# A state-space scan rewritten: scanning h + x·B, diagonals of B on VectorE, convolution taps on VectorE

## The chip, the core and the metric

The kernel runs on one core of a Trainium2 chip as a single launch. The metric is the device time of that launch in microseconds (us). The core's engines run side by side, each with its own queue in a fixed order: TensorE (PE; PEld is its weight load), VectorE (DVE), ScalarE (ACT), GpSimd (POOL), and SyncE (SP), which only issues DMA here. An engine that reaches an instruction whose input is not ready stands still, and so does everything behind it in its queue.

## What is computed

Two layers, each with a sequence mixer and a feed-forward part, over 8 sequences of 256 tokens with 128 features. Only the first mixer changes. It is a selective state-space block (D = 256 channels, N = 16 states per channel, K = 4 taps):

```python
Xn = layernorm(X)
X_main = Xn @ W_up1.T                                  # (b, l, 256)
X_main = silu(causal_depthwise_conv(X_main, conv_w, K=4) + conv_b)
pp = X_main @ W_ll.T + b_ll
delta = softplus(pp[..., :D]); Bm = pp[..., D:D+N]; Cm = pp[..., D+N:]
A = -exp(A_log)                                        # (D, N)
A_bar = exp(delta * A)
U = X_main * (A_bar - 1) / (delta * A) * delta * Bm    # = X_main * Bm * (A_bar - 1) / A
H[t] = A_bar[t] * H[t-1] + U[t]                        # for each of D x N states
Y[t] = sum over n of Cm[t, n] * H[t, :, n]
out = X + (Y * silu(Xn @ W_up2.T)) @ W_down.T + b_down
```

After it come an expert-choice feed-forward part (8 experts, 512 tokens each), a retention layer with 8 heads, and a top-2 feed-forward part over 16 weight banks.

## The kernel before, in words

**Setup.** x is loaded and normalized and turned into `XnT` (features on the partitions, tokens along the free axis, three zero columns ahead of each sequence). The convolution is folded into the up projection: GpSimd multiplies W_up1 by each tap into `wcv` (line 242), and the four products are added up by TensorE. `eye` is the 64-column identity in both halves of the partitions; `dg` holds diagonals of 1/A.

**front(q), lines 303 to 410,** prepares a block of two sequences (512 tokens), in pieces that `yield`. First the convolution: for each of two channel chunks `dc` and each sequence `h`, four matmuls into `pu` (L314), which ScalarE moves to `xm` (L318). Then the gate (L327), the projections for delta (L353, `pd`) and for B and C (L364, `pbc`), softplus through Exp and Ln, the transposed B (`pbt` L383 to `BT` L388) and the transposed x (`pxT` L393 to `xT` L401, and with its halves swapped by DMA, `xS`). Delta is put together by a subtraction on GpSimd (L406) and an addition on VectorE (L408), both with two operands in SBUF. C goes to DRAM and comes back broadcast over all partitions as `Cb` (L644).

**The loop over 64 units** (line 787 on) walks b (8 sequences), g (4 groups of 4 states) and dc (2 channel chunks). Each unit k is a tile of 128 channels x 4 states x 256 tokens, and passes through:

- `spread_b` (L657, GpSimd, one (b, g) ahead by four units): `Bd` = `eye` times B, two instructions for each (b, g), so that a matmul of x with it spreads x·B over the tokens
- `x_times_b` (L673, TensorE): 8 matmuls, x·B into PSUM as `u`
- `decays` (L684, ScalarE): `ab` = exp(delta·A), four instructions
- `steps` (VectorE): L692 makes `u` <- (ab - 1)·u, L694 writes zero into the first decay of each state, and L696 is one scan over all 4 x 256 elements, h <- ab·h + u
- `times_c` (L700, GpSimd): h <- h·C
- `sums` (L709, TensorE): 16 matmuls with `dg` add up the states over n, times 1/A, into `py`
- after 8 units: `gated` (L718, VectorE) and `down` (L726, L733, TensorE), to `ypr`

The order on PE, DVE, ACT and POOL is the order of the program, written out by hand. In iteration k: VectorE gets `steps(k)`; TensorE gets a part of the expert work, `x_times_b(k + 1)`, `sums(k - 2)`; GpSimd gets `times_c(k - 1)` and `spread_b` for unit k + 4 (if dc is 0); ScalarE gets `decays(k + 2)`. Then every generator in `running` gives one piece: `front(1)` to `front(3)` (started at units 0, 16 and 32 by `START`), the threshold search for the experts (`find`: L431 to L453 on VectorE and L444 on TensorE, ten rounds), the residual base (L772, L774 on GpSimd) and the selection of each expert's tokens (`select`: L522 to L531 on VectorE, L535 and L557 on TensorE, indirect gathers L548 on GpSimd). The expert work itself (L606, L624 on TensorE, L611, L629 on ScalarE, indirect scatters L572 on GpSimd) is cut into five parts an expert. `front(0)` runs entirely ahead of the loop, with five rounds of `find` between its pieces. `u` has 2 buffers in PSUM, `ab` 3, `h` 4, and all other matmul results share 2 banks (`bank`).

After the loop comes the second layer (lines 866 on), which the change does not touch.

Of the kernel before, what the change touches and what calls it, by code (L numbers as in the profile page):

```python
# [8 lines left out]
F32 = mybir.dt.float32  # L9
# [3 lines left out]
ALU = mybir.AluOpType  # L13
# [4 lines left out]
NB = 8  # L18
# [28 lines left out]
WB = DI + NH * DM + NH  # L47


@with_exitstack  # L50
def block_kernel(ctx: ExitStack, tc: tile.TileContext, a: dict, out: bass.AP):
# [33 lines left out]
    )  # L85
    ones_b = const.tile([P, P], BF16, name="ones_b")
# [63 lines left out]
    with ExitStack() as l0:  # L150
# [25 lines left out]
        wcv = main.tile([P, K, D], F32, name="wcv")  # L176
# [9 lines left out]
        for q in range(4):  # L186
# [3 lines left out]
        conv_w = main.tile([P, K, D], F32, name="conv_w", tag="Cb", bufs=3)  # L190
        nc.sync.dma_start(
            conv_w.rearrange("p k d -> p (k d)"),
            a["conv_w"].rearrange("k d -> (k d)").partition_broadcast(P),
        )
# [11 lines left out]
        wll = load0("wll", [P, ND, D + 2 * N], a["wll"].rearrange("(c p) e -> p c e", p=P))  # L206
        bll_d = load0("bll_d", [P, ND])
        bll_bc = load0("bll_bc", [2 * N, 1])
# [33 lines left out]
        nc.gpsimd.tensor_tensor(wcv, bc(wup1, 1, K), conv_w, ALU.mult)  # L242
# [58 lines left out]
        gate, delta, xT, BT = {}, {}, {}, {}  # L301

        def front(q):
            cols = slice(q * BLK, (q + 1) * BLK)
            win = slice(2 * q, 2 * q + 2)
            xq = main.tile([P, ND, BLK], F32, name=f"xm{q}", tag="xm")
# [3 lines left out]
            for dc in range(ND):  # L310
                for h in range(2):
                    pu = bank(f"pu{dc}_{h}_{q}", [P, L])
                    for k in range(K):
                        nc.tensor.matmul(  # L314
                            pu, wcv[:, k, dc * P : (dc + 1) * P], XnT[:, 2 * q + h, k : k + L],
                            start=(k == 0), stop=(k == K - 1),
                        )
                    nc.scalar.activation(  # L318
                        xq[:, dc, h * L : (h + 1) * L], pu, AF.Silu if q == 0 else AF.Identity,
                        bias=conv_b[:, dc : dc + 1],  # L320
                    )
                    yield
# [39 lines left out]
            pb = bank(f"pbc{q}", [2 * N, BLK])  # L362
            for kc in range(ND):
# [3 lines left out]
            BC = main.tile([2 * N, BLK], F32, name=f"BC{q}", tag="BC")  # L367
            nc.scalar.activation(BC, pb, AF.Identity, bias=bll_bc)
            nc.sync.dma_start(
                C_d[2 * q : 2 * q + 2].rearrange("b (n l) -> n b l", l=L),  # L370
                BC[N:, :].rearrange("n (b l) -> n b l", l=L),
            )
            yield
            nc.vector.scalar_tensor_tensor(z, w, -1.0, z, ALU.add, ALU.subtract)
# [12 lines left out]
            for rows, at in own:  # L387
                nc.scalar.copy(BTq[rows, :, at], pbt[rows, :, at])  # L388
            for i in range(2):
# [21 lines left out]


# [3 lines left out]
        ready, complete = set(), set()  # L416
# [12 lines left out]
        def search():  # L429
# [66 lines left out]
            G = main.tile([P, 2, NB, E0], F32, name="G")  # L496
# [153 lines left out]
        def spread_b(b, g):  # L650


            t = main.tile([P, 4, 2, BK], F32, name=f"Bd{b}_{g}", tag="Bd", bufs=3)
            j = 4 * (b % 2)
            for i in range(2):
                w = slice(2 * i, 2 * i + 2)
                nc.gpsimd.tensor_tensor(  # L657
                    t[:, w], eye.unsqueeze(1).unsqueeze(1).to_broadcast([P, 2, 2, BK]),
                    bc(BT[b // 2][:, j + 2 * i : j + 2 * i + 2, NG * g + 2 : NG * g + 4], 3, BK),
                    ALU.mult,  # L660
                )
            Bd[b, g] = t

        def x_times_b(k):

            b, g, dc = units[k]
            U[k] = ps_u.tile([P, NG, L], F32, name=f"u{k}", tag="u")
            for c in range(2):
                for half in range(2):
                    for r in range(2):  # L670
# [5 lines left out]
                            Bd[b, g][rows, 2 * c + half], start=True, stop=True,  # L676
                        )

# [10 lines left out]
        def steps(k):  # L689

            hh[k] = main.tile([P, NG, L], F32, name=f"h{k}", tag="h", bufs=4)
            nc.vector.scalar_tensor_tensor(U[k], ab[k], -1.0, U[k], ALU.add, ALU.mult)  # L692

            nc.vector.memset(ab[k][:, :, 0:1], 0.0)  # L694
# [757 lines left out]
```

## Time and profile before

| | |
|---|---|
| median of 3 runs | 685.59 us (685.58 to 686.54) |
| the profiled execution's own time | 684.96 us |
| its span in the trace | 683.1 us |
| PE busy | 544.8 us (80%), mean granted clock 0.873 |
| DVE busy | 432.2 us (63%) |
| POOL busy | 383.8 us (56%) |
| ACT busy | 332.3 us (49%) |
| first and last scan of the loop start at | 67.0 and 418.2 us |

The profile comes from one execution. A group of instructions shows how often it ran, its busy time, the mean of one in ns, and after the second bar how long its engine stood idle ahead of it and whom it waited for. A window row gives, for a stretch of the span, the busy time of each engine with the number of instructions, then the granted TensorE clock, the DMA share and GB/s. An fp32 matmul leaves two records, so L673 shows 1024 for 512 matmuls. Records of one engine can overlap: an instruction that is issued while its predecessor still runs begins, in the record, before it can work.

### The profile page before, as it was taken

Reading aid. Unit: us, or ns where it says so; the run is one execution under the profiler, and the core shown is the slowest. Engines: PE = TensorE matmul, PEld = TensorE weight load, DVE = VectorE, ACT = ScalarE, POOL = GpSimd, SP = SyncE. Lnnn points to the kernel's source line nnn. Section 1 sums busy time; section 2 is a strip of 40 time slices with the busy share of each in tenths; the row PEclk is TensorE's granted clock in tenths of the full one; section 3 lists DMA queues with packets and bytes.
Section 4 is the critical chain, followed back from the end, with each engine's and each line's share of the span. In section 5 each row is a group of like instructions: output and inputs, shape, how many; then the busy total and the mean of one; then the engine's idle time right before and its main releaser. Section 6 shows DMA issues by size and latency. Waiting matters only on the chain.

```text
span 683.1 us, 14527 instructions
## 1 busy us (share of the span) xinstructions
PE 544.8 (80%) x5721; PEld 415.7 (61%) x5721; DVE 432.2 (63%) x669; ACT 332.3 (49%) x763; POOL 383.8 (56%) x320
## 2 busy tenths in 40 slices
PE   0897768779989889979887975496449989999980
PEld 0665645667755668755766764354125589999870
DVE  7377898997955767856868696664027543544423
ACT  2646346447487756587764741362003244555430
POOL 5004565686988789987899896107730023344240
PEclk9996798889999899999999998577558899999995
DMA  7914101232396243332332220124224247889206
GB/s 203 117 25 124 33 32 40 104 95 82 73 204 138 74 115 73 95 93 66 95 91 55 71 71 6 62 93 139 110 81 148 84 151 252 264 292 312 88 30 186
DMA packets 59859, 76.27 MB, mean 112 GB/s; under 512 B 14992, under 2 KB 43808, under 8 KB 59536
## 3 DMA queue, kind: packets, MB, share of 16 engines
q1 hardware_dynamic: 51632, 65.81, 33.6%
q0 software_dynamic: 8160, 9.54, 6.6%
q8 instruction: 45, 0.74, 0.4%
q14 instruction: 22, 0.18, 0.1%
HBM read 59.46 MB, written 13.78 MB: 107 GB/s over the span
## 4 chain that ended last, share of the span: by engine, by line
PE 50%; DVE 20%; issue 9%; ACT 8%; POOL 4%; another core or an unknown queue 4%; DMA 3%; SPq 1%; POOLq 0%; DVEq 0%; ACTq 0%
PE ph L1201 5%; PE py L709 5%; PE py L1215 5%; PE u L673 5%; PE ph L606 4%; DVE h L696 4%; DVE u L692 4%; PE pu L314 4%; PE po L624 2%; PE ps L1034 2%; ACT ab L684 2%; PE pd L353 2%; POOL h L700 2%; DVE st L1041 1%
## 5 line engine op out<-in xcount | busy, mean ns | idle before, releaser
L700 POOL TENSOR_TENSOR h<-h,Cb 128x1024 f32<-128x1024 f32 x64 | 169.5, 2744 | 35.4 <-DVE h L696 20.1
L696 DVE TENSOR_TENSOR_SCAN h<-ab,u 128x1024 f32<-128x1024 f32 x64 | 146.3, 2287 | 5.9
L684 ACT ACTIVATE ab<-delta,An 128x256 f32<-128x256 f32 x256 | 108.5, 497 | 19.4 <-DVE h L696 17.5
L1221 POOL DMA_INDIRECT y_d<-yo,xt x47 | 45.5, 968 | 115.9 <-DVE yo L1220 103.8
L692 DVE SCALAR_TENSOR_TENSOR u<-ab,u 128x1024 f32<-128x1024 f32 x64 | 77.8, 1216 | 37.7 <-PE u L673 18.8
L709 PE MATMUL py<-h,dg 64*64 64x128 f32 x2048 | 79.0, 296 | 18.3 <-POOL h L700 11.3
L673 PE MATMUL u<-Bd,xT 64*128 64x128 f32 x512 | 81.1, 304 | 14.4 <-DVE h L696 12.7
L673 PEld LDWEIGHTS u<-Bd,xT 64*128 64x128 f32 x512 | 68.6, 206 | 25.2 <-issue 9.9
L709 PEld LDWEIGHTS py<-h,dg 64*64 64x64 f32 x2048 | 62.5, 145 | 33.0 <-POOL h L700 17.0
L673 PE MATMUL u<-Bd,xS 64*128 64x128 f32 x512 | 79.4, 305 | 1.7 <-DMA xS<-xT 1.7
L1206 ACT ACTIVATE hid<-ph,wb 128x128 f32<-128x128 f32 x188 | 53.3, 370 | 49.2 <-issue 24.0
L673 PEld LDWEIGHTS u<-Bd,xS 64*128 64x128 f32 x512 | 66.7, 206 | 2.0 <-DMA xS<-xT 2.0
L1041 DVE TENSOR_TENSOR st<-ps,decay_sb 128x384 f32<-128x384 f32 x64 | 31.2, 547 | 53.8 <-remote 27.7
L572 POOL DMA_INDIRECT acc_d<-oc,idx x32 | 51.5, 1609 | 17.0 <-ACT oc L629 8.8
L1150 POOL DMA_INDIRECT xs_d<-xk,pos x32 | 32.1, 1002 | 41.4 <-DVE hit L1132 31.9
L1201 PE MATMUL ph<-xT,wb 128*128 128x128 f32 x376 | 51.5, 281 | 3.3 <-DVE xT L1195 2.7
L657 POOL TENSOR_TENSOR Bd<-eye,BT 128x256 f32<-128x256 f32 x64 | 52.3, 1050 | 0.0
L1215 PE MATMUL py<-wb,hid 128*128 128x128 f32 x376 | 50.2, 278 | 0.0
L1201 PEld LDWEIGHTS ph<-xT,wb 128*128 128x128 f32 x376 | 46.6, 195 | 5.7 <-DVE xT L1195 3.1
L624 PE MATMUL po<-w,ht 128*128 128x128 f32 x256 | 39.5, 296 | 10.8 <-ACT BT L388 2.6
L624 PEld LDWEIGHTS po<-w,ht 128*128 128x128 f32 x256 | 33.7, 199 | 22.1 <-ACT ht L611 8.0
L1215 PEld LDWEIGHTS py<-wb,hid 128*128 128x128 f32 x376 | 46.4, 194 | 0.1
(257 smaller groups left out, 896.6 us busy)
## 6 DMA issues: line engine op xcount, KB each, us to landing
wb<-in_bank_dram SPq DMA_DIRECT2D x47, 514.0 KB
Cb<-C_d SPq DMA_DIRECT2D x32, 512.0 KB
w<-in_w_dram SPq DMA_DIRECT2D x16, 256.0 KB
xs_d<-zrow SPq DMA_DIRECT2D x1, 3031.5 KB
xt<-xs_d SPq DMA_DIRECT2D x11, 260.0 KB
xS<-xT SPq DMA_DIRECT2D x16, 128.0 KB
y<-y_d SPq DMA_DIRECT2D x8, 256.0 KB
decay_sb<-in_decay_dram SPq DMA_DIRECT2D x1, 1536.0 KB
```

Of the source, the lines that this page charges most:

```text
L572: i = nc.gpsimd.indirect_dma_start(out=acc_d, out_offset=bass.IndirectOffsetOnAxis(ap=idx[:, e, s : s + 1], axis=0), in_=oc, in_offset=Non ...
L624: nc.tensor.matmul(po, ht[:, hc, s * P : (s + 1) * P], w2[:, hc, :], start=(hc == 0), stop=(hc == NH - 1),)
L657: nc.gpsimd.tensor_tensor(t[:, w], eye.unsqueeze(1).unsqueeze(1).to_broadcast([P, 2, 2, BK]), bc(BT[b // 2][:, j + 2 * i : j + 2 * i + 2, ...
L673: nc.tensor.matmul(U[k][:, 2 * r : 2 * r + 2, t0 : t0 + BK], xT[b][r ^ half][rows, c, dc * P : (dc + 1) * P], Bd[b, g][rows, 2 * c + half] ...
L684: nc.scalar.activation(ab[k][:, n, :], delta[b // 2][:, dc, (b % 2) * L : (b % 2 + 1) * L], AF.Exp, scale=An[:, dc, g * NG + n : g * NG + ...
L692: nc.vector.scalar_tensor_tensor(U[k], ab[k], -1.0, U[k], ALU.add, ALU.mult)
L696: return nc.vector.tensor_tensor_scan(hf, af, uf, 0.0, ALU.mult, ALU.add)
L700: nc.gpsimd.tensor_mul(hh[k][:, w], hh[k][:, w], Cb[b, g][:, w])
L709: nc.tensor.matmul(pyv[cols, i, dc, :], dg[rows, dc, g * NG + n, :], hh[k][rows, n, j * P : (j + 1) * P], start=(g == 0 and dc == 0 and n ...
L1201: nc.tensor.matmul(ph[:, hc, :], w[:, hc * P : (hc + 1) * P], xTs[t], start=True, stop=True)
L1206: nc.scalar.activation(hids[t][:, hc, :], ph[:, hc, :], AF.Relu, bias=w[:, DI + NH * DM + hc : DI + NH * DM + hc + 1],)
L1215: nc.tensor.matmul(py, hids[t][:, hc, :], w[:, DI + hc * DM : DI + (hc + 1) * DM], start=(hc == 0), stop=(hc == NH - 1),)
```

## The change

It does three things, and moves some pieces to fit them.

1. **Scan.** With G = H + x·B the recurrence becomes G[t] = (G[t-1] + x[t]B[t] - x[t-1]B[t-1])·A_bar[t]. TensorE delivers the step differences directly: `Bd` is now made from `step` (the identity minus the identity shifted by one column), and two small extra matmuls for each unit (8 rows, 2x3 columns) subtract the step across the 64-token edges. `xE` holds what these need: 12 records of matmuls, two ScalarE copies and two small GpSimd products for each block. `steps` is now four scans of 256, add then multiply, with no L692 and no L694. What was added to H is taken out of Y once for each block: sum over n of C·B/A, times x, made by a VectorE product `CB`, a matmul `pq` and a VectorE product for each dc; four more matmuls of `sums` in each unit with g = 0 add it into `py`.
2. **Diagonals of B.** `spread_b` stays on GpSimd for the first 6 (b, g), and goes to VectorE for the other 26.
3. **Convolution.** One up projection (`wup1`, 512 columns) for each dc, and the four taps as four VectorE instructions that read `pu` from PSUM; the first has the bias. `wcv`, its GpSimd product and the broadcast load of the taps are gone.

The last piece of `front` (the `pq` piece) of block 0 runs in the loop; `front(1)` to `front(3)` start two units later; `pbc` has 48 rows rather than 32, so that C begins at row 32.

```diff
+    step = const.tile([P, BK], F32, name="step")
+    nc.vector.tensor_copy(step, eye)
+    nc.vector.tensor_sub(step[:, 1:], step[:, 1:], eye[:, 0 : BK - 1])
+    less = const.tile([P, BLK // BK], F32, name="less")
+    nc.vector.tensor_scalar(less, eye[:, 0 : BLK // BK], -1.0, None, ALU.mult)
...
-        nc.gpsimd.tensor_tensor(wcv, bc(wup1, 1, K), conv_w, ALU.mult)
...
             for dc in range(ND):
-                for h in range(2):
-                    pu = bank(f"pu{dc}_{h}_{q}", [P, L])
-                    for k in range(K):
-                        nc.tensor.matmul(
-                            pu, wcv[:, k, dc * P : (dc + 1) * P], XnT[:, 2 * q + h, k : k + L],
-                            start=(k == 0), stop=(k == K - 1),
-                        )
-                    nc.scalar.activation(
-                        xq[:, dc, h * L : (h + 1) * L], pu, AF.Silu if q == 0 else AF.Identity,
-                        bias=conv_b[:, dc : dc + 1],
+                pu = bank(f"pu{dc}_{q}", [P, BLK])
+                nc.tensor.matmul(
+                    pu, wup1[:, dc * P : (dc + 1) * P], XnT[:, win, K - 1 :],
+                    start=True, stop=True,
+                )
+                nc.vector.tensor_scalar(
+                    xq[:, dc, :], pu, conv_w[:, dc, K - 1 :], conv_b[:, dc : dc + 1],
+                    ALU.mult, ALU.add,
+                )
+                to, u = (t.rearrange("p (b l) -> p b l", l=L) for t in (xq[:, dc, :], pu))
+                for j in range(1, K):
+                    nc.vector.scalar_tensor_tensor(
+                        to[:, :, j:], u[:, :, 0 : L - j], conv_w[:, dc, K - 1 - j : K - j],
+                        to[:, :, j:], ALU.mult, ALU.add,
                     )
-                    yield
+                if q == 0:
+                    nc.scalar.activation(xq[:, dc, :], xq[:, dc, :], AF.Silu)
+                yield
...
+            CB = main.tile([N, BLK], F32, name=f"CB{q}", tag="CB")
+            nc.scalar.copy(CB, BC[CROW:])
...
+            nc.vector.tensor_mul(CB, CB, BC[0:N])
...
+            pe = bank(f"pe{q}", [P, D + N])
+            ends = [slice(r * BK, r * BK + BLK // BK) for r in range(2)]
+            for kc in range(ND + 1):
+                for rows in ends:
+                    xw = (xq[:, kc] if kc < ND else BC[0:N])[:, BK - 1 :: BK]
+                    nc.tensor.matmul(
+                        pe[rows, kc * P : min((kc + 1) * P, D + N)], xw,
+                        ident if kc < ND else ident[0:N, 0:N], start=True, stop=True,
+                    )
...
+            for rows in ends:
+                nc.scalar.copy(xe[rows], pe[rows])
+            for rows in ends:
+                nc.gpsimd.tensor_tensor(
+                    be[rows],
...
+            if q == 0:
+                pr = bank("prA", [N, D])
+                for dc in range(ND):
+                    nc.tensor.transpose(pr[:, dc * P : (dc + 1) * P], rA[:, dc, :], ident)
+                nc.scalar.activation(rAT, pr, AF.Copy, scale=-1.0)
+            for dc in range(ND):
+                pq = bank(f"pq{dc}_{q}", [P, BLK])
+                nc.tensor.matmul(
+                    pq, rAT[:, dc * P : (dc + 1) * P], CB, start=True, stop=True
+                )
+                nc.vector.tensor_mul(xq[:, dc, :], pq, xq[:, dc, :])
+            surplus.add(q)
+            yield
...
+            engine = nc.gpsimd if 4 * b + g < 6 else nc.vector
             for i in range(2):
                 w = slice(2 * i, 2 * i + 2)
-                nc.gpsimd.tensor_tensor(
-                    t[:, w], eye.unsqueeze(1).unsqueeze(1).to_broadcast([P, 2, 2, BK]),
+                engine.tensor_tensor(
+                    t[:, w], step.unsqueeze(1).unsqueeze(1).to_broadcast([P, 2, 2, BK]),
...
+            for r in range(2):
+                rows = slice(r * BK, r * BK + BLK // BK)
+                n = NG * g + 2 * r
+                nc.tensor.matmul(
+                    U[k][:, 2 * r : 2 * r + 2, BK:L:BK], xE[b // 2][0][rows, dc * P : (dc + 1) * P],
+                    xE[b // 2][1][rows, b % 2, n : n + 2, :], start=False, stop=True,
+                )
...
-            nc.vector.scalar_tensor_tensor(U[k], ab[k], -1.0, U[k], ALU.add, ALU.mult)
-
-            nc.vector.memset(ab[k][:, :, 0:1], 0.0)
-            hf, af, uf = (t.rearrange("p n l -> p (n l)") for t in (hh[k], ab[k], U[k]))
-            return nc.vector.tensor_tensor_scan(hf, af, uf, 0.0, ALU.mult, ALU.add)
+            for n in range(NG):
+                i = nc.vector.tensor_tensor_scan(
+                    hh[k][:, n, :], U[k][:, n, :], ab[k][:, n, :], 0.0, ALU.add, ALU.mult
+                )
+            return i
...
-            for n in range(NG):
+            assert b // 2 in surplus
+            for n in range(-1 if g == 0 else 0, NG):
                 for i, j in ((0, 0), (1, 1), (0, 1), (1, 0)):
                     rows, cols = slice(i * BK, (i + 1) * BK), slice(j * BK, (j + 1) * BK)
+                    if n < 0:
+                        w, t0 = eye[rows, :], (b % 2) * L + j * P
+                        src = xm[b // 2][rows, dc, t0 : t0 + P]
...
-        START = {0: front(1), 16: front(2), 32: front(3)}
+        START = {2: front(1), 18: front(2), 34: front(3)}
```

## The prediction

> **What bounds the kernel now.** I read the chain that ended last first, to see whether one engine sets the end. Its shares, by line:
>
> ```profile
> PE ph L1201 5%; PE py L709 5%; PE py L1215 5%; PE u L673 5%; PE ph L606 4%; DVE h L696 4%; DVE u L692 4%; PE pu L314 4%; PE po L624 2%; PE ps L1034 2%; ACT ab L684 2%; PE pd L353 2%; POOL h L700 2%; DVE st L1041 1%
> ```
>
> No line holds the end. L692 and L314, which the change removes or cuts, hold 4% each, some 26 and 25 us, but a chain's share is worth only what the next engine leaves of it. So I went to the groups:
>
> ```profile
> L700 POOL TENSOR_TENSOR h<-h,Cb 128x1024 f32<-128x1024 f32 x64 | 169.5, 2744 | 35.4 <-DVE h L696 20.1
> L696 DVE TENSOR_TENSOR_SCAN h<-ab,u 128x1024 f32<-128x1024 f32 x64 | 146.3, 2287 | 5.9
> ...
> L692 DVE SCALAR_TENSOR_TENSOR u<-ab,u 128x1024 f32<-128x1024 f32 x64 | 77.8, 1216 | 37.7 <-PE u L673 18.8
> L709 PE MATMUL py<-h,dg 64*64 64x128 f32 x2048 | 79.0, 296 | 18.3 <-POOL h L700 11.3
> ```
>
> The three engines of a unit wait for each other in a ring. Then the windows of the loop, to see how full each is (us, then PE, PEld, DVE, ACT, POOL busy, granted clock, DMA share, GB/s):
>
> ```profile
> 67.00:130.00 63.00, 48.86 (x494) 36.65 (x496) 57.76 (x78) 28.87 (x56) 35.10 (x25) 0.80 0.16 59
> 130.00:190.00 60.00, 51.79 (x746) 41.61 (x739) 50.97 (x51) 33.06 (x83) 50.60 (x40) 0.94 0.31 84
> 190.00:250.00 60.00, 51.29 (x625) 36.56 (x625) 37.14 (x36) 41.93 (x87) 49.01 (x35) 0.91 0.67 129
> 250.00:310.00 60.00, 55.37 (x711) 40.88 (x708) 43.14 (x43) 42.30 (x90) 53.53 (x43) 0.97 0.33 88
> 310.00:370.00 60.00, 53.02 (x712) 39.52 (x711) 45.04 (x42) 40.74 (x87) 52.63 (x39) 0.97 0.33 82
> 370.00:425.00 55.00, 41.95 (x704) 33.88 (x704) 42.47 (x37) 23.95 (x54) 46.48 (x28) 0.90 0.20 51
> ```
>
> Over these 358 us PE has 302, POOL 287 and DVE 276: almost level. Windows from one scan's start to the next show why (same columns):
>
> ```profile
> 160.15:166.84 6.69, 6.69 (x69) 4.96 (x68) 3.58 (x4) 5.86 (x12) 3.41 (x5) 1.00 0.36 121
> 181.77:185.41 3.64, 2.53 (x61) 2.21 (x63) 3.47 (x3) 2.67 (x9) 3.64 (x3) 1.00 0.22 23
> 414.54:418.18 3.64, 2.09 (x64) 1.60 (x64) 3.47 (x3) 0.00 (x0) 2.37 (x2) 1.00 0.00 0
> ```
>
> Units come in two kinds. Some 24 of 63 take 3.58 to 3.65 us, VectorE's own pace; units with expert or front work take 5 to 9 us, with PE full. The mean is 351/63 = 5.6 us.
>
> **The change part by part.**
>
> *Scan.* Before, back to back: 3.64 us a unit (row above). After, four scans of 256. One such scan stands in the trace:
>
> ```profile
> 458.00 0.68 DVE L1098 TENSOR_TENSOR_SCAN inc<-runs,mark 128x256 f32<-128x256 f32 x1
> ```
>
> The Trainium skill (VectorE: DVE Perf Modes, on the trn2 errata) says that the fixed cost is paid per instruction, and advises 512 elements or more; that speaks against cutting one scan into four. The rows give its size: 4 x 0.68 = 2.74 against 2.29. But a record begins some 0.09 us before its predecessor ends, so back to back I take 4 x 0.60 = 2.4 (bounds 2.4 and 2.75; that add-then-multiply runs at the same rate isn't shown). Gain 1.25 us a unit, 79 us of VectorE, but only on the path in VectorE-paced units.
>
> *Diagonals of B.* GpSimd loses 52 instructions. Recorded at 1050 ns, but pairs take 1.14 to 1.19 us together, so 0.59 each: 31 us off POOL. On VectorE one costs about 0.41 (L526, same size) or 0.33 back to back: 17 us. The real question is a lock. VectorE's product has both operands in SBUF, like L408:
>
> ```profile
> 132.50 1.20 DVE L408 TENSOR_TENSOR delta<-delta,w 128x1024 f32<-128x1024 f32 x1
> 234.71 3.69 DVE L408 TENSOR_TENSOR delta<-delta,w 128x1024 f32<-128x1024 f32 x1
> ```
>
> ```profile
> 132.72 3.19 POOL L700 TENSOR_TENSOR h<-h,Cb 128x1024 f32<-128x1024 f32 x1 [0.75 <-DVE h L696]
> 234.37 2.94 POOL L700 TENSOR_TENSOR h<-h,Cb 128x1024 f32<-128x1024 f32 x1
> ```
>
> At 132.5 VectorE was first and L700 took 3.19 instead of 2.37; at 234.7 L700 was first, ended at 237.31, and L408 then ran 1.1 us to 238.40. This is what the Trainium skill states (SBUF — State Buffer, on who interferes with whom): a VectorE instruction with two SBUF inputs and a GpSimd one that reads SBUF exclude each other for a whole instruction. By durations alone a pair costs VectorE 0.66; by the lock it depends on the moment. Both `Bd` instructions stand right behind scan k in VectorE's queue, and `times_c(k)` becomes ready at the end of that scan (L700 began 0.14 us behind it at 132.72). So the first gets in, GpSimd is next, and the second waits for a whole L700: 2.2 us. Behind it is queued scan k + 1, for which GpSimd, PE's sums and `u`'s buffer wait. Bounds: 0 (GpSimd late or both get in) and 4.6 us (both wait). I take 1.5 as the mean over 26 pairs, two of three paying (GpSimd works 287 of 358 us here, but a good part of it on gathers and scatters): 39 us.
>
> *Convolution.* PE loses 8 x 4 records of L314 a block, 7.7 us at full clock (1.93 per 8), and gets 4 records of 512 columns, 1.9 us (as 4 of L353 take 1.93): 17 us less for the three blocks in the loop. VectorE gets 8 instructions of 512 from PSUM, 0.69 each or 0.60 back to back (L718): 4.8 us a block, 14 in the loop. They stand between scans, and wait for `pu`, which PE makes at the end of its iteration; `pu` keeps one of two banks until the fourth tap.
>
> *Edges and surplus on PE.* Two edge matmuls are 4 records a unit. Nothing like them is in the trace; nearest is L383 (16 rows), 28 records in 1.57 us: 0.06 each, so 0.24 a unit, 15 us (bounds 0.1 and 0.5; no gain is possible, it is work added). `sums` of g = 0: 8 records of 0.034, 16 times, 4 us. `pe` 0.6 and `pq` 1.9 a block, `prA` once: 9 us. VectorE: `CB` 0.6 and `pq` 1.2 a block, 7 us. ACT: L318 away (4 x 0.47 a block), copies `CB` and `xe` instead: level, hidden. Loads of the taps and the 48 rows: hidden.
>
> Sums over the loop's 63 steps, from these durations at full clock: PE 278 -> 290; VectorE 263 -> 222, with the lock 261; POOL 31 less. Taking for each two neighbouring units the later of PE and VectorE (buffers allow one unit of slack) gives 309 before, where the loop took 351, and after 307 without the lock, 316 at 1.2 us a pair, 327 at 2.2. So about +10 at 1.5. The fuller queue of GpSimd cost something in the expert stretches (230 to 250, 300 to 320): I give back 4.
>
> *Ahead of the loop.* `wcv` held the lock for 2.3 us against L246 (2305 ns); gone, but `step`, `less` and the shift now queue against `dg` on the same lock: level. In `front(0)` the taps (4.8 us of VectorE) go ahead of search rounds whose counts PE's `pd` stands behind: `pd` 2 us later, with `pbt` and `pxT` behind it; `pe` adds 1.2 at half clock, and `be` waits for `xe` in front of delta's subtraction on GpSimd. Without L692 the first scan can end 1.3 earlier. Sum +3.
>
> The second layer (425 us on) has the same instructions: 0. Total: 684.96 + 10 - 4 + 3 = 694 in the profiled execution, 1.9 of it outside the span; the median lies 0.6 above that execution. I say 694.
>
> **The rivals.**
>
> *Main case, slower, 0.57:* VectorE's gain is eaten by the lock, PE gets 12 us more, and PE was full. 694 (687 to 706).
>
> *Faster, 0.28:* the chain is right, not the sums. L692 leaves it (26 us), three quarters of L314 (18 us), and the shorter scan answers the waits for L696 (20 us of POOL, 17.5 of ACT, 12.7 of PE). Its place are the 24 units at VectorE's pace and the ring of waits. If a quarter to a half of the 44 stays gained, and the lock is met mostly while VectorE would wait for PE anyway (under 0.5 us a pair on the path): 685 + 3 - 11 or - 22 gives 666 to 677; I say 673. Against it: PE has 2.4 to 3.9 us in most of them after the change, too.
>
> *Loads cancel, 0.07:* the lock costs 0.5 a pair: 685.
>
> *Both diagonals wait, 0.08:* 3 us a pair and more gives 338 for the paired sum: +29 + 3 - 4, so 713.
>
> The lock decides: at about 0.5 us a pair (paired sum 310, so +1 - 4 + 3) the change breaks even.
>
> **From these to numbers.** A measurement of this kernel can tell about 0.2% (1.4 us). Faster 0.28, same 0.06, slower 0.66. The range 672 to 709 leaves out the faster half of the faster case and most of the last. The main case alone is 687 to 706.
>
> **What would show it.** Right: `Bd` on VectorE with a mean over 1 us and second ones near 2.5; scans of 256 near 0.69; light units with a `Bd` longer than 3.64, those past the last `Bd` near 2.5; PE busy up by 10 to 15; first scan's end 2 to 4 us later. Wrong: `Bd` at 0.4; edge records far from 0.06; unit times in the expert stretches shorter than before.

## The result and the profile after

The changed kernel took 711.09 us (median of 4 runs, 709.60 to 715.38), 1.038 times the kernel before, with a 95% interval of 1.033 to 1.043. The forecast was 694.0 with a range to 709; the time lies above that range. The direction was right, the loss was three times the 8.4 us forecast. In the profiled executions the span went from 683.1 to 713.5 us: the first scan of the loop starts 8.7 us later (75.7), the 63 steps of the loop take 21.5 us more (372.6), the rest takes 265.2 instead of 264.9. The profiled execution of the changed kernel is the slowest of its four (715.38 us), so its profile shows some 4 us more than the median.

The chain that ended last, by line, on the page of the changed kernel:

```profile
PE py L779 6%; PE u L728 6%; PE ph L1271 5%; DVE h L757 5%; PE py L1285 5%; PE ph L657 4%; PE po L675 3%; PE ps L1104 3%; PE pd L363 3%; ACT ab L747 2%; DVE xm L326 2%; PE pret L1124 2%; PE pq L455 2%; PE u L737 2%; PE pg L337 1%
```

L692 (4%) and L314 (4%) are gone from it, as expected. In their place stand work that is new, L737 (edges), L455 (`pq`) and L326 (taps), 6% together, and more of L779 and L728. The chain has lost 8% and is no shorter: other work has taken the place. The groups of the page that answer to those shown of before:

```profile
L764 POOL TENSOR_TENSOR h<-h,Cb 128x1024 f32<-128x1024 f32 x64 | 169.7, 2714 | 46.3 <-DVE h L757 36.5
L757 DVE TENSOR_TENSOR_SCAN h<-u,ab 128x256 f32<-128x256 f32 x256 | 154.5, 667 | 34.3 <-PE u L737 29.3
...
L779 PE MATMUL py<-h,dg 64*64 64x128 f32 x2048 | 75.9, 286 | 10.9 <-POOL h L764 4.7
...
L710 DVE TENSOR_TENSOR Bd<-step,BT 128x256 f32<-128x256 f32 x52 | 47.9, 960 | 1.7 <-ACT BT L401 1.7
```

A scan is as short as forecast, but VectorE now waits 29.3 us for L737, the last of the matmuls that make `u`, where it waited 18.8 for L673, and GpSimd waits 36.5 us for VectorE where it waited 20.1. More of the waiting in the ring begins at PE. PE's own groups inside the loop, from the groups of that stretch:

```profile
L737 PE MATMUL u<-be,xe 8*128 8x6 f32 x256 | 26.5, 273 | 0.0
...
L455 PE MATMUL pq<-CB,rAT 16*128 16x512 f32 x16 | 12.2, 900 | 0.5 <-ACT rAT L452 0.5
...
L779 PE MATMUL py<-xm,eye 64*64 64x128 f32 x128 | 8.0, 323 | 7.2 <-DVE ge L486 3.8 <-DVE rr L582 2.7 <-DVE gate L786 0.7
```

The windows of the loop, cut at the scans of units 0, 9, 22, 30, 41 and 52, which start within 1.4 us of the cuts of before; columns as there:

```profile
75.68:140.41 64.73, 46.49 (x515) 31.95 (x513) 55.44 (x102) 28.98 (x57) 31.99 (x22) 0.79 0.14 50
140.41:206.00 65.59, 60.48 (x832) 46.25 (x832) 52.27 (x86) 33.45 (x84) 50.26 (x31) 0.87 0.30 87
206.00:268.43 62.43, 55.28 (x674) 38.18 (x672) 30.45 (x56) 42.23 (x84) 40.60 (x26) 0.93 0.60 113
268.43:335.25 66.82, 57.62 (x728) 41.71 (x732) 50.79 (x74) 41.08 (x90) 49.37 (x32) 0.94 0.32 81
335.25:403.46 68.21, 65.57 (x836) 49.36 (x828) 43.67 (x65) 42.69 (x92) 49.70 (x32) 0.92 0.31 75
403.46:455.08 51.62, 44.08 (x764) 36.67 (x764) 40.40 (x59) 23.93 (x54) 39.77 (x19) 0.93 0.19 50
```

They add up to PE 329.5, DVE 273.0 and POOL 261.7 us in 379.4, where before had 302, 276 and 287 in 358. PE is up by 27, although the convolution's 17 us have left it: some 44 us went in. Three units show the two kinds and a third:

```profile
178.49:183.59 5.10, 5.10 (x98) 4.50 (x91) 3.04 (x6) 4.62 (x13) 3.64 (x2) 1.00 0.15 16
...
363.67:376.25 12.58, 11.68 (x128) 8.52 (x120) 3.73 (x6) 3.56 (x12) 11.94 (x8) 0.85 0.42 91
...
435.31:437.64 2.33, 0.00 (x0) 0.00 (x0) 2.33 (x5) 0.00 (x0) 0.00 (x0) 0.91 0.01 4
```

The last row is the gain: a light unit at 2.33 instead of 3.64 us, and ten units run near that. The first is full of PE work, as before. In the second, a unit that took 3.6 us before, VectorE stands still while PE is busy for 11.7 of 12.6 us; VectorE's timeline says for what:

```profile
365.44 0.67 DVE L757 TENSOR_TENSOR_SCAN h<-u,ab 128x256 f32<-128x256 f32 x1
374.81 1.53 DVE L458 TENSOR_TENSOR xm<-pq,xm 128x512 f32<-128x512 f32 x2 [8.70 <-PE pq L455]
376.25 2.42 DVE L757 TENSOR_TENSOR_SCAN h<-u,ab 128x256 f32<-128x256 f32 x4
```

`pq` is the last thing that PE does in an iteration, and the product that reads it stands in VectorE's queue ahead of the next scan. It looks like a cause; an experiment below says what it is worth.

**Ahead of the loop.** PE's timeline of the changed kernel, and then of the kernel before:

```profile
42.81 0.21 PE L495 MATMUL pc<-cp,ones_b 128*128 128x56 bf16 x1 [4.57 <-DVE xm L326]
45.87 3.68 PE L337 MATMUL pg<-XnT,wup_sb 128*64 128x256 f32 x16 [2.86 <-DVE xm L326]
...
50.25 3.78 PE L363 MATMUL pd<-xm,wll_sb 128*128 128x512 f32 x4 [0.54 <-ACT gate L344]
...
55.39 3.43 PE L363 MATMUL pd<-xm,wll_sb 128*128 128x512 f32 x4 [1.31 <-ACT z L368]
```

```profile
45.35 1.95 PE L327 MATMUL pg<-XnT,wup_sb 128*64 128x256 f32 x16 [0.32 <-DVE keep L449]
47.23 1.98 PE L353 MATMUL pd<-xm,wll_sb 128*128 128x512 f32 x4
...
49.56 1.98 PE L353 MATMUL pd<-xm,wll_sb 128*128 128x512 f32 x4 [0.32 <-DVE keep L449]
```

Both shared banks hold a `pu` until its fourth tap is done, so PE stands idle for 4.57 and 2.86 us, with 0.21 us of work between, and then the same 16 matmuls take 3.68 instead of 1.95, and both `pd` 3.78 and 3.43 instead of 1.98. That is a factor of 1.7 to 1.9; the granted clock in these three stretches is 0.50, 0.50 and 0.57, where it is 1.00 before. The Trainium skill (TensorE: Matmul & The Clock Gate, Part 1) says that the clock halves after an idle window of about 3.4 us; the trace agrees, the first gap being longer than that. How long it lasts differs from run to run: in e1 and e2 below, with the same taps, the 16 matmuls take 3.61 and 3.35, but both `pd` 1.98 to 1.99, and the first scan starts at 72.7 and 72.1.

### The profile page after: what moved, and what is told of

Same layout as the page of the kernel before. It is cut to its first block, busy times and chain, and to the rows that moved or that the text cites. A ratio compares the mean times of both kernels' runs of the same rounds, so it can differ in the third digit from the quotient of the medians.

```text
span 713.5 us, 15256 instructions
## 1 busy us (share of the span) xinstructions
PE 570.6 (80%) x6059; PEld 425.5 (60%) x6059; DVE 432.8 (61%) x832; ACT 333.0 (47%) x762; POOL 355.8 (50%) x275
## 4 chain that ended last, share of the span: by engine, by line
PE 53%; DVE 21%; issue 10%; ACT 7%; POOL 4%; DMA 3%; SPq 1%; POOLq 0%; DVEq 0%; ACTq 0%
PE py L779 6%; PE u L728 6%; PE ph L1271 5%; DVE h L757 5%; PE py L1285 5%; PE ph L657 4%; PE po L675 3%; PE ps L1104 3%; PE pd L363 3%; ACT ab L747 2%; DVE xm L326 2%; PE pret L1124 2%; PE pq L455 2%; PE u L737 2%; PE pg L337 1%
## 5 line engine op out<-in xcount | busy, mean ns | idle before, releaser
L764 POOL TENSOR_TENSOR h<-h,Cb 128x1024 f32<-128x1024 f32 x64 | 169.7, 2714 | 46.3 <-DVE h L757 36.5
L757 DVE TENSOR_TENSOR_SCAN h<-u,ab 128x256 f32<-128x256 f32 x256 | 154.5, 667 | 34.3 <-PE u L737 29.3
L728 PE MATMUL u<-Bd,xT 64*128 64x128 f32 x512 | 84.7, 310 | 11.9 <-DVE h L757 9.6
L728 PEld LDWEIGHTS u<-Bd,xT 64*128 64x128 f32 x512 | 71.4, 211 | 25.7 <-issue 10.1
L779 PE MATMUL py<-h,dg 64*64 64x128 f32 x2048 | 75.9, 286 | 10.9 <-POOL h L764 4.7
L728 PE MATMUL u<-Bd,xS 64*128 64x128 f32 x512 | 82.8, 310 | 0.0
L779 PEld LDWEIGHTS py<-h,dg 64*64 64x64 f32 x2048 | 61.0, 140 | 17.5 <-issue 8.5
L728 PEld LDWEIGHTS u<-Bd,xS 64*128 64x128 f32 x512 | 69.4, 211 | 0.1
L710 DVE TENSOR_TENSOR Bd<-step,BT 128x256 f32<-128x256 f32 x52 | 47.9, 960 | 1.7 <-ACT BT L401 1.7
L675 PE MATMUL po<-w,ht 128*128 128x128 f32 x256 | 42.4, 311 | 7.2 <-ACT gate L346 2.7
L675 PEld LDWEIGHTS po<-w,ht 128*128 128x128 f32 x256 | 35.6, 210 | 19.6 <-ACT ht L662 6.0
L418 POOL TENSOR_TENSOR be<-less,xe 8x96 f32<-8x96 f32 x8 | 2.9, 363 | 82.5 <-ACT xe L416 82.1
```

The source lines that it names most:

```text
L675: nc.tensor.matmul(po, ht[:, hc, s * P : (s + 1) * P], w2[:, hc, :], start=(hc == 0), stop=(hc == NH - 1),)
L710: engine.tensor_tensor(t[:, w], step.unsqueeze(1).unsqueeze(1).to_broadcast([P, 2, 2, BK]), bc(BT[b // 2][:, j + 2 * i : j + 2 * i + 2, NG ...
L728: nc.tensor.matmul(U[k][:, 2 * r : 2 * r + 2, t0 : t0 + BK], xT[b][r ^ half][rows, c, dc * P : (dc + 1) * P], Bd[b, g][rows, 2 * c + half] ...
L757: i = nc.vector.tensor_tensor_scan(hh[k][:, n, :], U[k][:, n, :], ab[k][:, n, :], 0.0, ALU.add, ALU.mult)
L764: nc.gpsimd.tensor_mul(hh[k][:, w], hh[k][:, w], Cb[b, g][:, w])
L779: nc.tensor.matmul(pyv[cols, i, dc, :], w, src, start=(n < 0 and dc == 0), stop=(k % PER == PER - 1 and n == NG - 1),)
```

## The experiments

Six theories, in the order in which I held them. A: VectorE's wait for the lock of `Bd` (the forecast's). B: PE's added work, and VectorE waiting for results of the same iteration. C: part 1's own additions (edges; surplus, that is `pq` with its products and the sums with `eye`; and what feeds them: `pe`, `xe`, `be`, `CB`). D: the changed order of work. E: parts 2 and 3. F: in-order waits behind `be` and `pq`. Each ratio is to the kernel before on the same chip. The runs scan_only, no_edges, no_pq and gain_only had a chip on which the kernel before takes 649.32 us; the others, chips on which it takes 682.93 to 687.22.

**1. Diagonals without the lock** (e1_lockfree): the copy of `step` that VectorE reads lies in PSUM.

```diff
+        step_p = tab[:, 128 : 128 + BK]
+        nc.vector.tensor_copy(step_p, step)
...
-            engine = nc.gpsimd if 4 * b + g < 6 else nc.vector
+            engine, src = (nc.gpsimd, step) if 4 * b + g < 6 else (nc.vector, step_p)
...
-                    t[:, w], step.unsqueeze(1).unsqueeze(1).to_broadcast([P, 2, 2, BK]),
+                    t[:, w], src.unsqueeze(1).unsqueeze(1).to_broadcast([P, 2, 2, BK]),
```

> The changed kernel, but the 26 pairs of diagonals on VectorE read step from a copy in PSUM, so that only one operand lies in SBUF; same instructions, same place in the queue. Theory A (the lock between VectorE and GpSimd is the cause): the 52 products fall from a mean of 960 ns to about 0.4 us, the time from 711 to 690 or less. Theory B (PE's added work and VectorE's waits for results that PE makes at the end of the same iteration, taps behind pu and products behind pq, are the cause): the products get short, too, but the time falls by at most 5 us, to 706 to 711.

707.59 us, 1.0327 (1.0290 to 1.0364). The groups of its VectorE:

```profile
L712 DVE TENSOR_TENSOR Bd<-py,BT 128x256 f32<-128x256 f32 x52 | 19.5, 417 | 85.7 <-PE py L781 60.8 <-PE pyo L803 13.7 <-remote 11.2
```

The mean of a `Bd` falls from 960 to 417 ns, so the lock held VectorE for 28 us in all (52 x 0.543), 1.1 us a pair. But only 3.5 us come back, within the intervals, and the row says why the run doesn't price the lock: the copy lies in the tile of `py`, and now the `Bd` instructions wait for PE's `py`, 60.8 us together. One wait was taken away and another put in. Inconclusive alone; e2 and e16 decide.

**2. All diagonals on GpSimd** (e2_bd_pool): `engine = nc.gpsimd`.

> The changed kernel with all diagonals of B on GpSimd, as before. Theory A: 690 or less, as no product of VectorE stands behind a lock. Theory B: 706 to 716, GpSimd gets its 31 us back and VectorE loses waits that lay beside PE's work.

711.19 us, 1.0422 (1.0352 to 1.0493). No gain: with the lock gone and 28 us more work on GpSimd, the time is the same within the intervals.

**3. The convolution back on PE** (e3_conv_pe), in two pieces: `wcv`, L314 and L318 as before, the taps gone.

> The changed kernel with the convolution back on PE (four matmuls per sequence from wcv, ScalarE moves pu to xm). Theory A: PE gets 17 us of work more in the loop, the time stays at 711 or rises. Theory B: the first scan starts 5 us or more earlier than 75.7, the units 2, 3, 18, 19, 34 and 35 lose their waits, and the time falls by 12 to 20, to 691 to 699.

707.68 us, 1.0345 (1.0301 to 1.0390). The first scan starts at 70.1 us instead of 75.7, but the whole is only 3 us better, within the intervals. Theory B's 12 to 20 us did not come: part 3 isn't the loss. Nor is it a gain, for the 17 us of work that PE gets back here cost nothing that these ratios can tell.

**4. Surplus products one piece later** (e4_pq_split):

```diff
                 pq = bank(f"pq{dc}_{q}", [P, BLK])
...
+                if q:
+                    yield
                 nc.vector.tensor_mul(xq[:, dc, :], pq, xq[:, dc, :])
```

> The changed kernel with the two pq products of blocks 1 to 3 each one iteration behind their matmul, so that VectorE doesn't wait for a matmul at the end of the same iteration; same instructions. Theory A: no change, 711. Theory B: the wait of L458 for pq (19.2 us) goes for blocks 1 to 3 and units 10, 29 and 45 get shorter; the time falls by 4 to 12, to 699 to 707; if PE's work alone holds those units, the wait moves to the next scan and the time stays.

726.29 us, 1.0602 (1.0556 to 1.0648): 15 us worse than the change. Neither theory had that. VectorE waits 4.8 us for `pq` instead of 19.2, but one of the two shared banks is held over an iteration, PE's groups wait 6.9 us for the product in the two rows below, and VectorE's wait for L739, the edges of this run, goes from 29.3 to 44.4:

```profile
L677 PE MATMUL po<-w,ht 128*128 128x128 f32 x256 | 41.7, 308 | 13.2 <-ACT tk L595 3.5 <-DVE xm L460 3.4 <-ACT gate L346 2.8
...
L796 PE MATMUL pyo<-wdown_sb,gate 64*128 64x128 f32 x120 | 12.2, 319 | 5.0 <-DVE xm L460 3.5 <-DVE gate L788 1.2
```

**5. Part 1 alone** (e5_scan_only): e2 and e3 together.

> Part 1 alone: the new scan with its edges and its surplus, the diagonals all on GpSimd and the convolution on PE. If the three parts each cost something of their own (theory A and B mixed), undoing two of them brings the sum of what they brought singly (711.2 and 707.7 against 711): about 705 to 708. Theory C (part 1's own additions to PE, edges and pq with their waits, are the whole cause, and parts 2 and 3 are neutral): also 703 to 708. If parts 2 and 3 only hide each other (each undone alone uncovers the other): 690 or less.

676.43 us against 649.32, 1.0410 (1.0347 to 1.0473). Part 1 alone costs as much as the whole change.

**6 and 7. The change without edges** (e6_no_edges: L737 left out) **and without surplus** (e7_no_pq: `pq`, its product and the sums with `eye` left out).

> The changed kernel without the two edge matmuls of each unit (leaves out the correction across the 64-token edges; everything else stays). L737 is busy 26.5 us in the trace and stands right in front of the scan that waits for it. Theory C: 20 us or more come back, 685 to 691. Theory B (what counts is the work of the front pieces, with pq and the two-unit later start): at most 10, 701 or more.

> The changed kernel without the pq piece: no matmul pq, no products behind it, no four extra matmuls of sums with g = 0 (leaves out taking the surplus C*B/A*x from Y). Theory B: VectorE's 19.2 us of waits for pq and 20 us of PE's records go, and the time falls by 15 or more, to 696 or less. Theory C in its edges: by 8 or less, 703 or more.

1.0329 (1.0265 to 1.0394) and 1.0378 (1.0315 to 1.0441). Neither gives back what it occupies on PE: neither C's 20 us for the edges nor B's 15 for the surplus came.

**8. The gain alone** (e8_gain_only): the kernel before, with L692 and L694 left out and its scan replaced.

```diff
-            nc.vector.scalar_tensor_tensor(U[k], ab[k], -1.0, U[k], ALU.add, ALU.mult)
-            nc.vector.memset(ab[k][:, :, 0:1], 0.0)
-            return nc.vector.tensor_tensor_scan(hf, af, uf, 0.0, ALU.mult, ALU.add)
+            for n in range(NG):
+                i = nc.vector.tensor_tensor_scan(
+                    hh[k][:, n, :], U[k][:, n, :], ab[k][:, n, :], 0.0, ALU.add, ALU.mult)
+            return i
```

> The kernel before with its steps alone changed: four scans of add then multiply for L692, L694 and L696, and nothing added anywhere (leaves out the factor a - 1 and the steps' differences, so it scans something else, in the same shapes). This is the gain of the change without any of its price. The prediction's sums say that it is small (paired sums of PE and VectorE fall by 13 or so, the light units being held by PE at 2.4 to 3.9 us): 665 to 675. If the chain's shares were right, 640 to 660.

637.45 us, 0.9777 (0.9690 to 0.9865). VectorE is relieved of 67 us (DVE 364.8 busy after 432.2), and 2.2% of the time comes of it.

**9 to 12, on one chip.** e9_after_again is the changed kernel; e10_plan_only has e8's gain in the changed order of work (convolution on PE); e11_scan_old_plan is part 1 in the order of before:

```diff
-FRONT = 9
+FRONT = 11
...
-        START = {2: front(1), 18: front(2), 34: front(3)}
+        START = {0: front(1), 16: front(2), 32: front(3)}
...
-                first_unit = k + 14
+                first_unit = k + 16
```

with a `yield` after each sequence of the convolution; e12_old_plan_no_edges is e11 without L737.

> The changed kernel once more, on the chip of the three runs beside it, so that each of them has its own reference here. Expected by every theory: 1.038 times the kernel before, 1.033 to 1.043. First scan about 8.5 us later than before, the 64 units about 20 us longer, the stretch after them equal.

> The gain of the scan alone (four add-multiply scans a unit, as in the run gain_only) in the changed kernel's order of work: the convolution in two pieces on PE, the fronts of the next pairs started at units 2, 18 and 34 instead of 0, 16 and 32, fewer and denser pieces. It leaves out the edge matmuls, the surplus products and their sums with eye, the products C*B and the transposes for the edges, so y isn't the reference's. Theory D, the order of work costs: it stays near the changed kernel, 1.015 to 1.03 times before, though none of the additions is in it. Theory C, the additions of part 1 cost: 0.975 to 0.985 times before, as in the run gain_only. In between: both.

> Part 1 with all of its additions (edges, surplus, sums with eye, step differences on GpSimd), in the order of work of the kernel before: convolution on PE in four pieces, eleven pieces a front, fronts started at units 0, 16, 32. The full result. Theory D (order of work): 0.985 to 1.01 times before, some 25 us below the run scan_only's ratio of 1.041. Theory C (additions): 1.035 to 1.045, as scan_only.

> The same as the run scan_old_plan, without the two edge matmuls of each unit, so the state's own first steps of each stretch of 64 are left out of u. Theory C: 15 to 17 us (0.24 to 0.26 us a unit) below scan_old_plan. Theory D: below it by 5 us or less, since the edges lie beside other waits once the order of work is the old one.

1.0341 (1.0262 to 1.0421); 0.9838 (0.9762 to 0.9915); 1.0277 (1.0187 to 1.0366); 1.0093 (1.0069 to 1.0116). Theory D falls as the main cause: without the additions, the changed order is still faster than before, though e11 lies 0.006 below e9 and 0.013 below e5, with intervals that overlap. C holds in the main: either order loses with the additions in it, though e11 lies below C's range and above D's.

**13. Edges of zeros in the kernel before** (e13_before_zero_edges):

```diff
+            for r in range(2):
+                nc.tensor.matmul(
+                    U[k][:, 2 * r : 2 * r + 2, BK:L:BK], zx[rows, dc * P : (dc + 1) * P],
+                    zb[rows, b % 2, n : n + 2, :], start=False, stop=True)
```

> The kernel before with one thing added: the two edge matmuls of each unit (8 rows, 2 states by 3 steps), fed with tiles of zeros, so that the full result is unchanged. Theory C (an addition to PE costs what it holds PE): slower by 13 to 16 us, 1.018 to 1.024 times before. Rival (in the kernel before a unit is bound by VectorE's 3.64 us in the light stretches, so the edges are hidden there, and cost only in the stretches where PE leads): 5 to 9 us, 1.007 to 1.013.

701.97 us, 1.0218 (1.0159 to 1.0278): 15 us for the edges alone, without any other change. Their row:

```profile
L687 PE MATMUL u<-zb,zx 8*128 8x6 f32 x256 | 26.3, 271 | 0.0
```

Of 26.3 us of records, 15 are on the path by the medians, 0.23 us a unit. In the traces the loop takes 362.1 us instead of 351.2, 10.9 more or 0.17 a unit; most of the rest of the profiled difference lies behind the loop, where the instructions are the same.

**14 and 15. Part 1 in the old order without surplus** (e14_old_plan_no_pq), **and without surplus and edges** (e15_old_plan_neither).

> The run scan_old_plan without the surplus: the two pq matmuls and products of each pair of batches and the sums with eye are left out (h is summed with the surplus still in it), the edges are kept. Theory C: 1.005 to 1.012 times before, 11 to 15 us below scan_old_plan's 1.028, since pq and the eye sums hold PE for 16 to 20 us and some of it is hidden. Rival (the edges hide the surplus's cost, or it lies in waits that stay): 1.02 or more.

> The run scan_old_plan without the edges and without the surplus (both left out of the result); the transposes for the edges, the products C*B and the step differences stay. Theory C, with costs that add up: edges 13 and surplus 14 us below 1.028, so 0.985 to 0.993 times before. If the two cover each other: above 1.0, or below 0.98 if the transposes and C*B cost nothing.

1.0194 (1.0121 to 1.0267) and 0.9989 (0.9956 to 1.0023). Point values give: edges 0.0205 without surplus and 0.0184 with it (e12 to e11), surplus 0.0104 without edges and 0.0083 with them. In this order the two add up, though the 0.0083 alone is not clear of the intervals. e14's own expectation was too low, because I had put the surplus as high as the edges.

e15 is above its expectation of 0.985 to 0.993, too, and that shows a third cost. It has the order of work of e8 (0.978) and differs from it by what feeds the additions: `pe`, `xe`, `be`, `CB`, `step` for `eye` and 48 rows of `pbc`. These feeders cost 0.021 (0.012 to 0.031), measured on two chips; against e10 (0.984), which has the changed order but a chip with the time of e15's, it is 0.015. In the traces the loop takes 328.9 us in e8 and 348.0 in e15. Units 12 to 27 take 88.0 and 88.3; nearly all of the difference lies in units 8 and 9, 28 to 31 and 44 to 51, and each of these stretches begins where GpSimd stands in front of `be`. First e15's waits, then two instructions of VectorE and two of PE in units 30 and 31:

```profile
POOL be L418 <- ACT xe L416: 23.6, 3, 9.0
```

```profile
229.93 1.23 DVE L444 TENSOR_TENSOR delta<-delta,w 128x1024 f32<-128x1024 f32 x1 [5.64 <-POOL delta L442]
...
243.61 2.43 DVE L739 TENSOR_TENSOR_SCAN h<-u,ab 128x256 f32<-128x256 f32 x4 [5.96 <-PE u L717]
```

```profile
237.68 1.62 PE L761 MATMUL py<-h,dg 64*64 64x128 f32 x32 [3.05 <-POOL h L746]
...
245.56 1.98 PE L761 MATMUL py<-h,dg 64*64 64x128 f32 x32 [2.72 <-POOL h L746]
```

GpSimd stands still for 8.8 us until 226.66. Then its part of delta and its products h·C come late, PE's sums wait for these and VectorE for PE: the two units take 15.5 us instead of 6.8. That the whole 0.021 comes this way is argued from the traces; no run moved `be` in this order.

**16. The whole change without part 1's additions** (e16_after_neither). Parts 2 and 3 and the changed order stay.

> The changed kernel without part 1's additions: no edges, no surplus, no transposes for the edges, no C*B (left out of the result), but with the diagonals on VectorE, the taps on VectorE and the changed order of work. Theory C: leaving out edges alone or surplus alone gave back 0 to 8 us because each covers the other and the lock; with both gone it falls to 0.99 to 1.005 times before. Theory E (parts 2 and 3 and the order of work hold the loss): it stays at 1.02 or more, against 0.984 for the run plan_only, which has the same order of work without parts 2 and 3.

674.21 us, 0.9790 (0.9725 to 0.9855), which is below C's range. Theory E falls, and A with it, as this group of e16 shows:

```profile
L674 DVE TENSOR_TENSOR Bd<-step,BT 128x256 f32<-128x256 f32 x52 | 50.1, 1004 | 2.5 <-ACT BT L398 2.5
```

The lock is met as often as in the changed kernel, and the time is 2.1% below before.

**17 and 18. The waits mended.** In the changed kernel GpSimd stands 7.5 to 10.4 us behind `be` three times in the loop, and VectorE 19.2 us behind `pq`. e17_be_next_piece moves the two `be` products behind the next `yield`; e18_be_pq_next_piece also lets ScalarE empty the bank of `pq` at once, and VectorE multiply one piece later:

```diff
-                nc.vector.tensor_mul(xq[:, dc, :], pq, xq[:, dc, :])
+                nc.scalar.copy(z[:, dc, :], pq)
+            yield
+            nc.vector.tensor_mul(xq, z, xq)
```

> The changed kernel, full result, with one instruction pair moved: GpSimd's two products be (L418), which stand in the same piece of the front as the PE transposes and ScalarE copies that they wait for, go into the next piece. Theory F (part of the loss is GpSimd's queue standing still behind be, 7.5 to 10.4 us each time, three times in the loop, with h*C of the next unit behind it): GpSimd's wait for xe goes from some 27 us in the loop to under 3, and the time falls by 6 to 14 us, to 1.014 to 1.028 times before. Rival (GpSimd would have waited for the scan anyway; only the PE's own work counts): the wait is taken over by h*C waiting for the scan, and the time stays at 1.032 to 1.038.

> As be_next_piece, and the surplus products are taken off their PE wait too: ScalarE copies pq out of its bank in the same piece, and VectorE multiplies from there one piece later. Full result. Theory F: VectorE's 19 us of waiting for pq in the loop goes to under 3, and the time falls by another 5 to 10 us below be_next_piece. Rival (the scans behind the product would have waited for PE anyway, and ScalarE takes the wait over, with the decays ab behind it): equal to be_next_piece within 3 us.

704.90 us, 1.0350 (1.0291 to 1.0409), and 704.01 us, 1.0326 (1.0268 to 1.0384). The 6 to 14 us that theory F had for `be` did not come in the medians, nor the 5 to 10 for `pq`. Both waits are gone, and VectorE's waits of e17 and of e18 in the loop show where the second went:

```profile
DVE h L757 <- PE u L737: 31.0, 11, 6.6
...
DVE xm L458 <- PE pq L455: 12.6, 6, 6.2
```

```profile
DVE h L759 <- PE u L739: 40.8, 14, 5.7
```

31.0 + 12.6 before the move, 40.8 after it: the scan would have waited for PE anyway. A stall of 8.7 us that is plain to see in a timeline was worth nothing that these runs can tell.

For `be` it is less clear. e17 and the change differ by 0.003, with room for a gain of some 7 us, and GpSimd's wait for the scan did not take the wait over (35.1 us after 36.5; 12.4 us went to `z`). The loop takes 361.9 us in e17's trace, 372.6 in the change's and 373.0 in e9's; but e17's profiled execution is the fastest of its six, and the other two are the slowest of their four.

## Why the prediction was wrong

Put together, in ratios to the kernel before, each row with one thing more than the row above:

| | ratio | from |
|---|---|---|
| the gain of the scan alone | 0.978 | e8 |
| and what feeds the additions | 0.999 (+0.021) | e15 |
| and the surplus | 1.009 (+0.010) | e12 |
| and the edges | 1.028 (+0.018; alone: +0.022) | e11 (e13) |
| and parts 2 and 3 with their order of work: the change | 1.034 to 1.038 (+0.006 to +0.010, not clear of noise) | e9, the result |

All of the loss is part 1's additions: with everything else in place, e16 stands at 0.979, and 0.979 to 1.038 is 40 us.

**The step that failed** is "Edges and surplus on PE" with the sum made of it, "PE 278 -> 290". I put 15, 4 and 9 us on PE, 28 in all, and took 17 off for the convolution. Two terms of it were wrong.

- *The feeders.* `pe` had 0.6 us a block, the copies `CB` and `xe` were "hidden", and a wait of GpSimd for `xe` was named only ahead of the loop. They cost 0.015 to 0.021, 10 to 14 us (e15 against e10 and e8), and in e15 GpSimd stands 5.7 to 9.0 us in front of `be` three times in the loop.
- *The offset.* Part 3 as a whole, 17 us off PE and the taps on VectorE, gained nothing that these runs can tell: 1.038 with it and 1.0345 without (e3); without part 2, 1.0422 with it and 1.0410 without (e2, e5). So the 17 us did not stand against the additions in the time.

The edges and the surplus cost about what I had for them or less, but by the path and not by the work. In the loop's windows PE rises by 27 us, not 12; the records of edges (26.5), `pq` (12.2, forecast 7.6) and the sums with `eye` (8.0) alone are 46.7. On the path the edges cost 11 to 15 us (forecast 15) and the surplus about 7 (forecast 12). In all, the additions took 40 us from the time where the sum had 12 on PE.

**The lock** was the main case, and it was wrong. It did occur: the mean of `Bd` was 0.96, just under the "over 1 us" I named (min 394 and max 3926 ns), and the pure wait about 1.1 us a pair, 1.5 forecast. The Trainium skill's rule (SBUF — State Buffer, on who interferes with whom) agrees with it and with the 417 ns of e1, where one input lies in PSUM. But the order that I argued from was the rarer one: the second of a pair waited in four of 26 (2.57 to 3.93 us), the first in nine (1.06 to 3.64). And its price was wrong: I put 12 us of the paired sum on it (307 to 319), and e16 carries the same lock at 0.979, no worse than e10 with the diagonals on GpSimd (0.984; the intervals overlap). So the wait must lie mostly where VectorE would have waited anyway; for what, these runs don't show. That the direction came out right is luck: the mechanism that I gave for it costs nothing that they can tell, and the loss came by a term that I had at under half its size.

**Ahead of the loop**, forecast +3, measured +8.7 in the profiled execution. I wrote that `pu` keeps a bank until the fourth tap, but did not follow that both banks are then held at once, nor that idle PE comes back at half the clock. With the convolution on PE (e3) the first scan starts at 70.1. Some 3 of the 8.7 us belong to the longer spell at half the clock in that execution (72.7 and 72.1 in e1 and e2).

**What held.** The scan: 667 ns each (0.69 forecast), 2.42 us for four, against 2.4; cutting the scan in four cost 0.13 us over the 2.29 of one. Light units (27 before, where I counted 24) without a `Bd` at 2.33 to 2.44, near the 2.5 I named; but units 14 and 20, with a `Bd`, took 3.00 and 2.99, not above 3.64, because neither of the pair waited (0.40 and 0.42 us each; GpSimd's L764 began with the second). GpSimd fell by 28.0 us (31 forecast). The second layer did not change (264.9 and 265.2). The forecast's faster rival named the size of the gain well: 666 to 677, and e16 gave 674.2. What it left out were the additions.

**What stays open.** In the changed order the costs of the parts can't be told one by one: leaving out edges or surplus alone gives back 0 to 0.005 (e6, e7), leaving out both and their feeders 0.059 (e16). The traced loops of e6 and e7 are 15 and 14 us shorter than the change's, but these two were the fastest of their runs and the change's was the slowest of its. The feeders alone were not run in that order, and whether GpSimd's wait in front of `be` costs anything there isn't settled (e17). For VectorE's wait for `pq`, e18 gives no sign that it costs anything. Why VectorE loses nothing by the lock stays open as well.

No version with the full result beat the kernel before: the best, e11, stands at 1.028.

## What to carry over

When two engines end the waits in turn, price a change by the work it puts on each, and first of all on the one that is full in the heavy units: here 2% gained on VectorE was paid for with 6%, half of it for two kinds of matmuls on PE and a third for the small instructions that feed them. Small work has a queue, too: a pair of `be`, 0.8 us of work, held GpSimd's queue for 5.7 to 9.0 us at a time. And a saving on an engine counts only if a run shows that it reaches the time. Measure the price of an addition alone, with zeros, in the old kernel, before writing the rest. A visible stall is worth its length only if nothing else would have waited there: take it away and look at who waits next before calling it a cause.

## What the hardware showed

The two edge matmuls of a unit, 8 rows and 6 columns each, leave four records of 0.27 us that lie over one another and over their neighbours, and cost 0.17 to 0.23 us a unit. After gaps of 4.57 and 2.86 us PE ran the next matmuls 1.7 to 1.9 times slower, at a granted clock of 0.50 to 0.57. A VectorE product of two SBUF operands took up to 3.93 us beside GpSimd's, and 0.39 to 0.43 with one operand in PSUM. And on one chip the kernel before took 649.32 us instead of some 686; the part after the loop alone was about 30 us shorter there in every kernel whose trace I have, so only ratios on one chip compare.
